# A two-layer graph network on one Trainium2 core: the adjacency loaded and turned by halves of its rows, score rows loaded ahead of W, the first norm's factor put into the exponentials, a PSUM bank for each half at the end

## The chip, the core and the metric

The kernel runs on one core of one Trainium2 chip. The core has five engines with a queue of instructions each, carried out in order: TensorE (PE in the profile; it multiplies a loaded 128x128 matrix with a stream of columns and also transposes), VectorE (DVE), ScalarE (ACT), GpSimd (POOL) and SyncE (SP). They wait for each other through semaphores. DMAs are issued from the queues of SP, ACT and POOL and land some microseconds later. Tiles live in on-chip memory with 128 partitions; PE writes into PSUM, here eight banks of 128x512 float32.

The metric is the time of one execution on the device in microseconds. Before the change it is 1136.07 us, the median of three runs (1135.92 to 1138.34).

## The reference

Batch of 32, 512 nodes, 128 features, one adjacency for all. Layer 0 is an attention over neighbours, layer 1 a gated recurrence of five steps with the same adjacency on both of its inputs. Cut to what matters:

```python
# layer 0
h = max(layernorm(x), 0)
hw = h @ W
e_src, e_dst = hw @ a_src, hw @ a_dst
logits = leaky_relu(e_src[:, :, None] + e_dst[:, None, :], 0.2)
alpha = softmax(logits + where(A > 0, 0, -1e9), axis=-1)
x = x + leaky_relu(alpha @ hw + b, 0.3)
# layer 1
h = max(layernorm(x), 0)
for step in range(5):
    m = A @ h                       # the same for "in" and "out"
    av = concat([m, m])
    u3 = h @ u3_w.T + u3_b
    z = sigmoid(av @ w3_w.T + w3_b + u3)
    r = sigmoid(av @ w4_w.T + w4_b + u3)
    hv = tanh(av @ w5_w.T + w5_b + (r * h) @ u5_w.T + u5_b)
    h = (1 - z) * h + z * hv
x = x + h
```

## The kernel before

**Tiling.** A batch is one tile of 128 partitions x 4 x 128 (`K` = 4 rows of nodes on each partition: node `4p + k`). The adjacency is turned once, into `adjT`, half precision, 128 x 4 x 512. One loop in Python makes all work as a list of tasks: for every batch `layer0(b)`, then `recurrence(b, step, ...)` for the five steps.

**What sets the order.** The kernel carries its own planner, `plan` (L88). Each task names its engine, its estimated duration (`COST`), a due time (`key`), what it needs and the buffers it takes. The planner always takes, among the tasks that can begin first, the one with the earliest key, and the instructions of each engine are then issued in that order and pinned to it. So a key, an estimate or a landing time (`ADJ_LANDS` and the `lands=` arguments) changes the order, never the waits themselves, which semaphores make. Instructions outside tasks (constants, some loads) are not pinned and are placed by the framework's own scheduler. Fillers (`idle`, L442) are matmuls on constants that nobody reads: `FIRST_IDLE` = 27 from the start, `FILL` = 8 from 6.15 us and `IDLE` = 36 from 6.5 us in the planner's time, which it takes where no other PE task can begin.

**The start.** SP issues x of batch 0 (L401), a_dst as a column (L412), the adjacency in one DMA of 1 MB (L415), x of batches 1 and 2, then the weights (L422 and on). ACT's queue issues W (`gw`, L407) and a_src as a column (L408). PE turns W (L456) and multiplies it with both score vectors (`wa_ps`, L463); ACT writes the results as three extra columns of `wrow` (L468 to L471). `prepare_adjacency(c)` (L486) transposes four 128x128 blocks of the landed adjacency into a bank, for `c` = 0 to 3, and ACT or DVE copies the bank into `adjT[:, c]` (L503).

**Layer 0 of a batch.** `relu_layernorm` (L602): statistics on DVE (L621, L629, L630), the power -1/2 on POOL (L650, `rs`), for batch 0 centring and scaling on DVE (L659, L665), for the others one ACT activation for each 128 columns (L687). Turning: `transposed` on PE (L707) with an ACT copy (L712) for the first four batches (`direct`), `blockwise` with a DVE transpose and DMAs on POOL's queue (L729 to L752) for the rest. `product` (L803): h times `wrow` (`hp`, L812), exponentials of the extra columns on ACT (L818), scaling of h·W by the exponential (L825). The row of scores is spread over partitions by PE transposes (`es`, L847) for the first four batches and by DMAs (L872, L885) for the rest. `weigh` (L894) makes the weights `pt` on DVE (L897); for batch 0 this goes by halves of 256 columns (`HALVED`). `average` (L921) multiplies them with h·W on PE (`av`, L928), and DVE normalizes and joins (L955 to L982). A second norm and turn follow (`hN`, `t_b`), and the halves `hi` and `lo` in half precision (L1012, L1014).

**A step of the recurrence** (L1018): `m` from `adjT` with `hi` and `lo` (L1037, 8 matmuls of 128x512), copied by ACT (L1048); r gate (L1056, L1057), tanh on ACT (L1062), r·h on DVE (L1069); z gate (L1077, tanh L1089); candidate (L1100, L1101, tanh L1107); three DVE updates (L1114, L1120, L1123); and the way back to node order, by DMA transposes on SP's queue (L1245), by PE, or by DMAs through memory.

**The last step of the last batch** (`ending`, L1256) goes by two halves of 256 columns: candidate (L1288), tanh (L1295), gated product (L1299), a turn that adds the kept part and the new part in PSUM (`minus`, L1276, and `plus`, L1306), sum with x1 (L1314), store (L1322). Both halves share one bank for the candidate (`v_end`) and one for the turned result (`end`).

**The guard.** A flag that inputs keep the fast path's bounds is computed late and read by every engine (L1350) before the last `BRANCH` = 150 tasks.

## Time and profile before

| what | value |
|---|---|
| median of the runs | 1136.07 us (1135.92 to 1138.34, 3 runs) |
| profiled execution | 1138.11 us |
| its span, first to last instruction | 1136.3 us |
| granted PE clock, mean | 0.999 |
| DMA moved | 104.52 MB |
| adjacency, issue to landing | 7.8 us |
| x of a batch, issue to landing, median | 2.9 us |

The rows of the profile are: an engine's busy time (the union of its instructions' times), groups of equal instructions with their mean duration, and a timeline in which a row "10.06 0.87 DVE L621 ..." gives start, duration, engine, line and tiles; in square brackets stands how long the engine was idle before it and what ended that. Matmuls are pipelined and their ends are modelled: a 128x128 float32 transpose is shown with 0.27 us, but the next one starts 0.11 us later, and a 128x512 float32 product is two rows 0.43 us apart. So PE's time is read from starts. Fillers count as busy.

### The profile page before, as it was taken

What the parts mean: (1) busy time and instruction counts of PE and PEld (TensorE: products, weight loads), DVE (VectorE), ACT (ScalarE), POOL (GpSimd) and SP (SyncE); (2) the same over time, 40 slices, a digit from 0 to 9 for tenths busy, and PEclk for the clock granted to TensorE, in tenths of its full rate; (3) what the DMA queues carried; (4) which work ended last, traced back from release to release, by engine and by line L of the source; (5) the groups of instructions that cost most, each with busy time, mean ns of one, the idle gap of its engine ahead of it and who ended that gap; (6) DMA issues with size and microseconds to landing.
All of it is one profiled execution on the core that took longest, in us unless ns stands there. A gap on an engine that the chain in (4) does not pass through costs nothing.

```text
span 1136.3 us, 14341 instructions
## 1 busy us (share of the span) xinstructions
PE 1128.5 (99%) x4337; PEld 593.3 (52%) x4337; DVE 875.9 (77%) x2002; ACT 661.4 (58%) x1299; POOL 352.3 (31%) x504
## 2 busy tenths in 40 slices
PE   8999999999999999999999999999999999999998
PEld 7665554555455545555545554555555554444444
DVE  7889868887687688779777777889888977655655
ACT  5756656645655565656565556665665565545553
POOL 4255542511421344244134214453644221100000
PEclk9999999999999999999999999999999999999999
DMA  3255454543434553454445444545555343231321
GB/s 107 57 84 104 84 113 89 110 105 74 112 75 97 98 121 76 96 125 103 93 94 105 79 91 111 112 100 110 127 113 103 76 75 84 47 74 29 84 74 67
DMA packets 188498, 104.52 MB, mean 92 GB/s; under 512 B 152192, under 2 KB 167680, under 8 KB 188288
## 3 DMA queue, kind: packets, MB, share of 16 engines
q1 hardware_dynamic: 170512, 66.57, 25.8%
q0 software_dynamic: 17472, 36.79, 17.5%
q8 instruction: 36, 0.59, 0.2%
q14 instruction: 46, 0.38, 0.1%
q10 hardware_dynamic: 432, 0.20, 0.1%
HBM read 39.46 MB, written 30.47 MB: 62 GB/s over the span
## 4 chain that ended last, share of the span: by engine, by line
PE 99%; DMA 1%; DVE 0%; SPq 0%; issue 0%; DVEq 0%
PE m L1037 24%; PE g L1077 12%; PE g L1057 12%; PE g L1056 12%; PE v L1100 12%; PE v L1101 12%; PE av L928 10%; PE hp L812 3%; DMA a_sb<-in_adj_dram 1%; PE idle L443 0%; PE at_ps L494 0%; PE t_b L707 0%; PE es L847 0%; PE t_a L707 0%; PE v_end L1288 0%; PE end L1306 0%
## 5 line engine op out<-in xcount | busy, mean ns | idle before, releaser
L1062 ACT ACTIVATE rs<-g,zrb 128x512 f32<-128x512 f32 x160 | 109.6, 685 | 123.1 <-PE g L1057 122.6
L1114 DVE SCALAR_TENSOR_TENSOR d<-hv,hT 128x512 f32<-128x512 f32 x158 | 108.3, 685 | 93.9 <-ACT hv L1107 92.8
L1107 ACT ACTIVATE hv<-v,vb 128x512 f32<-128x512 f32 x159 | 108.9, 685 | 108.2 <-PE v L1101 108.0
L1069 DVE SCALAR_TENSOR_TENSOR rh<-rs,hT 128x512 f32<-128x512 f32 x160 | 109.4, 685 | 70.5 <-ACT rs L1062 69.8
L1056 PE MATMUL g<-hT,u3T 128*128 128x512 f32 x320 | 163.4, 592 | 0.0
L1057 PE MATMUL g<-mT,w4sT 128*128 128x512 f32 x320 | 163.4, 592 | 0.0
L1077 PE MATMUL g<-mT,w3dT 128*128 128x512 f32 x320 | 162.8, 593 | 0.0
L1100 PE MATMUL v<-mT,w5sT 128*128 128x512 f32 x318 | 162.4, 592 | 0.0
L1101 PE MATMUL v<-rh,u5hT 128*128 128x512 f32 x318 | 162.4, 592 | 0.0
L1037 PE MATMUL m<-adjT,hi 128*128 128x512 f16 x640 | 162.1, 379 | 0.0
L1037 PE MATMUL m<-adjT,lo 128*128 128x512 f16 x640 | 160.7, 379 | 0.0
L650 POOL TENSOR_TENSOR rs_b<-ve_b,mhalf 128x4 f32<-128x4 f32 x32 | 37.0, 1155 | 383.0 <-DVE ve_b L630 184.5
L1089 ACT ACTIVATE zs<-g,zrb 128x512 f32<-128x512 f32 x160 | 109.4, 685 | 67.9 <-PE g L1077 66.4
L1048 ACT COPY mT<-m 128x512 f32<-128x512 f32 x160 | 92.8, 583 | 81.5 <-PE m L1037 79.0
L928 PEld LDWEIGHTS av<-hw,pt 128*128 128x128 f32 x1024 | 123.5, 191 | 21.1 <-issue 17.5
L928 PE MATMUL av<-hw,pt 128*128 128x129 f32 x1024 | 125.0, 275 | 0.1
L1123 DVE SCALAR_TENSOR_TENSOR hT<-d,hT 128x512 f32<-128x512 f32 x158 | 109.3, 692 | 11.9
L1237 ACT CAST hiT<-hT 128x512 f16<-128x512 f32 x128 | 78.9, 616 | 63.7 <-DVE hT L1123 63.2
L1037 PEld LDWEIGHTS <-hi 128*128 128x128 f16 x640 | 62.5, 98 | 99.0 <-issue 45.3
L1120 DVE SCALAR_TENSOR_TENSOR d<-zs,d 128x512 f32<-128x512 f32 x158 | 109.2, 691 | 5.2
L1037 PEld LDWEIGHTS <-lo 128*128 128x128 f16 x640 | 62.6, 98 | 90.5 <-issue 25.3
L1240 DVE TENSOR_TENSOR loT<-hT,hiT 128x512 f16<-128x512 f32 x128 | 87.7, 687 | 17.7 <-ACT hiT L1237 16.4
(141 smaller groups left out, 1354.1 us busy)
## 6 DMA issues: line engine op xcount, KB each, us to landing
x<-in_x_dram SPq DMA_DIRECT2D x32, 256.0 KB, 2.9
out_dram<-res SPq DMA_DIRECT2D x31, 256.0 KB, 2.3
turn_a<-blocks_a POOLq DMA_DIRECT2D x112, 64.0 KB, 2.6
h0T<-turn_a POOLq DMA_DIRECT2D x28, 256.0 KB, 4.0
es<-line POOLq DMA_DIRECT2D x28, 256.0 KB, 3.9
turn_b<-blocks_b POOLq DMA_DIRECT2D x112, 64.0 KB, 2.6
hT<-turn_b POOLq DMA_DIRECT2D x28, 256.0 KB, 3.8
way<-blocks SPq DMA_DIRECT2D x28, 256.0 KB, 2.3
```

Of the source, the lines that this page charges most:

```text
L928: pin(nc.tensor.matmul(avs()[:, i, :], lhsT=f_pts[c].tile[:, ts(2 * part + i, P)], rhs=hw()[:, c, : D + 1], start=start, stop=(c == K - 1) ...
L1037: pin(nc.tensor.matmul(f_m.tile, lhsT=part[:, k, :], rhs=adjT[:, k, :], start=(first and k == 0), stop=(not first and k == K - 1),))
L1056: pin(nc.tensor.matmul(g, lhsT=u3T, rhs=hT, start=True, stop=False))
L1057: pin(nc.tensor.matmul(g, lhsT=w4sT, rhs=f_mT.tile, start=False, stop=True))
L1062: pin(nc.scalar.activation(new(f_r, f"rs_{b}_{step}"), f_g.tile, AF.Tanh, bias=rb, scale=0.5))
L1069: pin(nc.vector.scalar_tensor_tensor(new(f_rh, f"rh_{b}_{step}"), f_r.tile, 1.0, hT, ALU.add, ALU.mult))
L1077: pin(nc.tensor.matmul(f_g.tile, lhsT=w3dT, rhs=f_mT.tile, start=False, stop=True, skip_group_check=True))
L1089: pin(nc.scalar.activation(new(f_z, f"zs_{b}_{step}"), f_g.tile, AF.Tanh, bias=zb, scale=0.5))
L1100: pin(nc.tensor.matmul(v, lhsT=w5sT, rhs=f_mT.tile, start=True, stop=False))
L1101: pin(nc.tensor.matmul(v, lhsT=u5hT, rhs=f_rh.tile, start=False, stop=True))
L1120: pin(nc.vector.scalar_tensor_tensor(d, f_z.tile, 1.0, d, ALU.add, ALU.mult))
L1123: pin(nc.vector.scalar_tensor_tensor(hT, f_d.tile, 0.5, hT, ALU.mult, ALU.add))
```

## The change

The adjacency is loaded by two DMAs, `k` = 0, 1 and `k` = 2, 3 of each partition; x of batch 1 is issued between them. `prepare_adjacency` now transposes, for each half of the rows, two pairs of column blocks, and the copies fill half-width parts of `adjT`. The weights `pt` need only the parts that they read.

The score vectors are loaded as two rows of one tile (`avecs`), issued on ACT's queue ahead of W. A matmul with a constant 2x4 matrix `pick` turns them into four columns (`acols`: a_dst, 0.8 a_src, -0.8 a_dst, a_src), which one product with W's transpose turns into the columns of `wrow`, 16 equal columns each, read back by one ACT copy. `pick` is made by four DVE operations from the identity, outside the planner's tasks.

For batch 0 the first norm is only centred and clipped; its factor `rs` goes into the exponentials as their scale and, times the exponential, into the scaling of h·W. The two halves of batch 0's turned h and of its spread scores have a bank each.

Batch 3's scores are spread and its second norm is turned by DMA now (`DIRECT_E`, `DIRECT_B` = 3). There are 24 fillers instead of 71. In the planner, PE's tasks before 6 us count double, `EARLY` is 7, keys of single tasks are shifted by a table, and landing times are others. The flag is read before the last 110 tasks.

At the end each half has its own bank for the candidate and for the turned result; the gated product is written over `hv`; the stores change queues; the z gate of the last batch no longer stands ahead of batch 30's candidate.

```diff
+DIRECT_A, DIRECT_E, DIRECT_B = 4, 3, 3
...
+SAME = 16
...
-EARLY = 6
+EARLY = 7
...
-ADJ_LANDS = 5600
+ADJ_LANDS = (4100, 5650)
+X_LANDS = (2800, 4450, 6250)
+X_FIRST = 1
+HALF_CLOCK = 6000
...
+BY_DVE = (1, 3)
+UNSCALED = 1
...
+BY_MATMUL = (0, 1)
+Z_AHEAD = 0
+SHIFT = {
+    ('adj', 0): 15.5, ('adj', 3): -1.0, (0, 0, 'step'): 1.5, (0, 18): 2.5, (0, 2, 'step'): -2.0,
...
+}
...
-FIRST_IDLE, FILL, IDLE = 27, 8, 36
+FIRST_IDLE, IDLE = 24, 0
...
-BRANCH = 150
+BRANCH = 110
...
-    acols = prep.tile([P, 2], F32, name="acols")
+    avecs = prep.tile([2, D], F32, name="avecs")
+    acols = prep.tile([P, 4], F32, name="acols")
+    pick = prep.tile([2, 4], F32, name="pick")
+    for i, (row, by) in enumerate(((1, 1.0), (0, 0.8), (1, -0.8), (0, 1.0))):
+        nc.vector.tensor_scalar(
+            pick[:, i : i + 1], ident[0:2, row : row + 1], by, None, ALU.mult
+        )
...
+    weights_0 = prep.tile([P, K], F32, name="weights_0")
...
+    nc.scalar.dma_start(out=avecs[0:1, :], in_=g_asrc.rearrange("(o d) -> o d", o=1))
+    nc.scalar.dma_start(out=avecs[1:2, :], in_=g_adst.rearrange("(o d) -> o d", o=1))
     nc.scalar.dma_start(out=gw, in_=g_w)
-    nc.scalar.dma_start(out=acols[:, 0:1], in_=g_asrc.rearrange("(d o) -> d o", o=1))
...
     def load_rest(name):
-        if name == "a_dst":
-            pin(nc.sync.dma_start(out=acols[:, 1:2], in_=g_adst.rearrange("(d o) -> d o", o=1)))
-            return
-        if name == "a":
-            pin(nc.sync.dma_start(out=a_sb, in_=adj.rearrange("(p k) m -> p k m", k=K)))
+        if isinstance(name, int):
+            ks = slice(2 * name, 2 * name + 2)
+            pin(nc.sync.dma_start(
+                out=a_sb[:, ks, :], in_=adj.rearrange("(p k) m -> p k m", k=K)[:, ks, :]
+            ))
             return
...
+    xs = {0: load_x(0, -9.9e9, X_LANDS[0])}
+    a_loaded = [add("SP", [1], -9.7e9, lambda: load_rest(0), lands=ADJ_LANDS[0])]
+    if X_FIRST:
+        xs[1] = load_x(1, -9.65e9, X_LANDS[1])
+    a_loaded.append(add("SP", [1], -9.6e9, lambda: load_rest(1), lands=ADJ_LANDS[1]))
+    if not X_FIRST:
+        xs[1] = load_x(1, -9.55e9, X_LANDS[1])
+    xs[2] = load_x(2, -9.5e9, X_LANDS[2])
+    rest_loaded = add("SP", [1] * 6, -9.45e9, lambda: load_rest("rest"), (xs[2][1],), lands=3000)
...
-    for n, columns, at in ((FIRST_IDLE, 480, 500), (FILL, 60, 6150), (IDLE, 256, 6500)):
-        for _ in range(n):
...
+    f_ac = Buffer("o", "bank")
     def issue():
-        pin(nc.tensor.matmul(new(f_wa, "wa_ps")[:, 0:2], lhsT=gwT, rhs=acols, start=True, stop=True))
-    t = add("PE", [256], soon, issue, (a_dst_loaded, t), (f_wa,), at=5000)
+        pin(nc.tensor.matmul(
+            new(f_ac, "ac_ps")[:, 0:4], lhsT=avecs, rhs=pick, start=True, stop=True
+        ))
+    u = add("PE", [256], soon, issue, (), (f_ac,), at=4200)
+    u = add("ACT", [1], soon, lambda: pin(nc.scalar.copy(acols, f_ac.tile[:, 0:4])), (u,), (f_ac,))
...
-        pin(nc.scalar.copy(wrow[:, D : D + 1], f_wa.tile[:, 1:2]))
-        pin(nc.scalar.mul(wrow[:, D + 1 : D + 2], f_wa.tile[:, 0:1], 0.8))
-        pin(nc.scalar.mul(wrow[:, D + 2 : D + 3], f_wa.tile[:, 1:2], -0.8))
-        pin(nc.scalar.copy(wa, f_wa.tile[:, 0:2]))
-    wrow_made = wa_made = add("ACT", [1] * 4, soon, issue, (t, w_copied), (f_wa,))
+        pin(nc.tensor.matmul(
+            new(f_wa, "wa_ps")[:, : 4 * SAME].rearrange("p (i q) -> p i q", i=4), lhsT=gwT,
+            rhs=acols.rearrange("p (i o) -> p i o", o=1).to_broadcast([P, 4, SAME]), start=True,
+            stop=True,
+        ))
...
+    t = add("PE", [256], soon, issue, (u, t), (f_wa,), at=0)
...
+    def issue():
+        pin(nc.scalar.copy(wrow[:, D : D + 4], f_wa.tile[:, 0 : 4 * SAME : SAME]))
+    wrow_made = add("ACT", [1], soon, issue, (t, w_copied), (f_wa,))
...
-    def prepare_adjacency(c):
+    def prepare_adjacency(i):
...
-        t = add("PE", [256] * K, key, turn, (a_loaded,), (f,), at=9900 if c > 1 else 0)
-        engine, copy = ("DVE", nc.vector.tensor_copy) if c % 2 else ("ACT", nc.scalar.copy)
-        adjacency.append(
-            add(engine, [512], key, lambda: pin(copy(adjT[:, c, :], f.tile)), (t,), (f,))
-        )
+            new(f, f"at_ps{i}")
+            for k in range(2):
+                for c in range(2):
+                    pin(nc.tensor.transpose(
+                        parts()[:, c, k, :],
+                        a_sb[:, 2 * two + k, :].rearrange("p (q c) -> p c q", c=K)[:, 2 * cs + c, :],
+                        ident,
+                    ))
+        t = add("PE", [256] * K, key, turn, (a_loaded[two],), (f,))
+        engine, copy = ("DVE", nc.vector.tensor_copy) if i in BY_DVE else ("ACT", nc.scalar.copy)
+        adjacency.append(add(
+            engine, [512], key,
+            lambda: pin(copy(
+                adjT[:, 2 * cs : 2 * cs + 2, ts(two, N // 2)],
+                f.tile.rearrange("p (c n) -> p c n", c=2),
+            )),
+            (t,), (f,),
+        ))
...
+            def centre(half):
+                def issue():
+                    for k in (2 * half, 2 * half + 1):
+                        pin(nc.vector.tensor_scalar(
+                            dst()[:, k, :], src()[:, k, :], own["mv"][:, k, 0:1], 0.0,
+                            ALU.subtract, ALU.max,
+                        ))
+                return issue
+            factor.append((own, t))
+            return [add("DVE", [128] * 2, keys(2), centre(i), (t1,), buffers) for i in range(2)]
...
-        f = Buffer("o", "bank")
+        fs = [Buffer("o", "bank")] * 2
+        if by_halves:
+            fs[1] = Buffer("o", "bank")
...
+            two = slice(2 * half, 2 * half + 2)
             def exponentials():
-                pin(nc.scalar.activation(
-                    hw()[:, 2 * half : 2 * half + 2, D:], hp2()[:, :, D:], AF.Exp
+                if unscaled:
+                    for k in range(2 * half, 2 * half + 2):
+                        pin(nc.scalar.activation(
+                            hw()[:, k, D:], hp2()[:, k - 2 * half, D:], AF.Exp,
+                            scale=norm["rs"][:, k : k + 1],
+                        ))
+                    return
+                pin(nc.scalar.activation(hw()[:, two, D:], hp2()[:, :, D:], AF.Exp))
+            def weight():
+                by = norm["rs"][:, two].rearrange("p (k o) -> p k o", o=1)
+                pin(nc.vector.tensor_tensor(
+                    weights_0[:, two].rearrange("p (k o) -> p k o", o=1), hw()[:, two, D : D + 1],
+                    by, ALU.mult,
                 ))
             def scale():
                 for c in range(2):
                     k = 2 * half + c
-                    pin(nc.scalar.mul(hw()[:, k, :D], hp2()[:, c, :D], hw()[:, k, D : D + 1]))
...
+                    by = weights_0[:, k : k + 1] if unscaled else hw()[:, k, D : D + 1]
+                    pin(nc.scalar.mul(hw()[:, k, :D], hp2()[:, c, :D], by))
...
+        if b < DIRECT_E:
+            f_ess = [Buffer("g", "bank")] * 2
+            if by_halves:
+                f_ess[1] = Buffer("o", "bank")
...
+                es_made.append(add("PE", [256] * 2, keys(0), spread(half),
+                                   (made[half], *es_made[-1:]), (f_hw, f_ess[half])))
...
-        def weigh(c, of, key):
+        def parts_of(of, c):
+            return [adjacency[2 * i + c // 2] for i in range(2) if of.start < N // 2 * (i + 1)
+                    and of.stop > N // 2 * i]
...
+            return add("DVE", [of.stop - of.start], key, issue,
+                       (es_made[half], made[c // 2], *parts_of(of, c)), (f_es, f_hw, f_pts[c]))
...
         t = turn(lambda: hTs[b % SLOTS], hN, f"b{b}", keys, t, (f_hN,), False)
-        return halved, t[0] if direct else t
+        return halved, t[0] if b < DIRECT_B else t
...
         if b >= B - LEVEL:
             key = min(key, (5 * B - EARLY - LEVEL * (STEPS - 1 - step)) * STEP)
+        key += SHIFT.get((b, step, "step"), 0) * STEP
...
-        if last and b == B - 1:
+        if Z_AHEAD and last and b == B - 1:
...
+            f = Buffer("o", "bank") if i else f_v
+            by_matmul = i in BY_MATMUL
+            f_end = Buffer("o", "bank") if by_matmul else f
+            of = slice(ks.start * P, ks.stop * P)
+            width = of.stop - of.start
...
             def candidate():
-                v = f_v.tile or new(f_v, f"v_{b}_end")
+                v = new(f, f"v_{b}_end_{i}")
                 for w, src in ((w5sT, f_mT), (u5hT, f_rh)):
...
             def gated():
-                p = f_p.tile or new(f_p, f"gated_{b}")
+                hv = f_hv.tile[:, of]
                 pin(nc.vector.scalar_tensor_tensor(
-                    p[:, ts(i, M)], f_z.tile[:, ts(i, M)], 1.0, f_hv.tile[:, ts(i, M)], ALU.add,
-                    ALU.mult,
+                    hv, f_z.tile[:, of], 1.0, hv, ALU.add, ALU.mult
                 ))
...
+            def turn_kept():
+                new(f_end, f"end_{b}_{i}")
+                for k in range(ks.start, ks.stop):
+                    pin(nc.tensor.matmul(
+                        f_end.tile[:, ts(k - ks.start, P)], lhsT=f_d.tile[:, ts(k, P)], rhs=minus,
+                        start=(k == ks.start), stop=False, skip_group_check=True,
+                    ))
...
-                    ))
+                for k in range(ks.start, ks.stop):
+                    if by_matmul:
+                        pin(nc.tensor.matmul(
+                            f_end.tile[:, ts(k - ks.start, P)], lhsT=f_hv.tile[:, ts(k, P)],
+                            rhs=plus, start=False, stop=True, skip_group_check=True,
+                        ))
...
             def result():
                 res = f_res.tile or new(f_res, f"res_{b}", (P, K, D))
-                ks = slice(two * i, two * i + two)
-                pin(nc.vector.tensor_tensor(
-                    res[:, ks, :], f.tile.rearrange("p (k d) -> p k d", k=K)[:, ks, :],
-                    x1s[b % SLOTS][:, ks, :], ALU.add,
+                pin(nc.vector.scalar_tensor_tensor(
+                    res[:, ks, :], f_end.tile[:, :width].rearrange("p (k d) -> p k d", d=D),
+                    1.0 if by_matmul else 0.5 / LIFT, x1s[b % SLOTS][:, ks, :], ALU.mult, ALU.add,
...
             def store():
-                ks = slice(two * i, two * i + two)
-                queue = nc.sync if i else nc.scalar
+                queue = nc.scalar if STORES[i] == "ACT" else nc.sync
                 pin(queue.dma_start(out=out_r[b][:, ks, :], in_=f_res.tile[:, ks, :]))
...
+            pieces.append(u)
+            key = ENDING_KEY + i
+            u = add("ACT", [width], keys(4 + key), tanh_v, (u,), (f, f_hv))
...
+            if by_matmul:
+                kept = add("PE", [512] * n, keys(-1), turn_kept, (t_keep, pieces[0]), (f_end, f_d))
+                u = add("DVE", [width], keys(4 + key), gated, (u, t_z), (f_z, f_hv))
+                u = add("PE", [512] * n, keys(4 + key), turn, (u, kept), (f_end, f_hv))
...
+            u = add("DVE", [width], keys(5 + key), result, (u,), (f_end, f_res))
+            add(STORES[i], [350 if STORES[i] == "ACT" else 1], keys(5 + key), store, (u,),
+                (f_res,), lands=LANDING)
```

## The prediction

> **What bounds the kernel now.** I read the engine totals and the chain that ended last, then the timeline of the first 40 us, then the load rates by stretch, then the end of the chain.
>
> ```profile
> span 1136.3 us, 14341 instructions
> ...
> PE 1128.5 (99%) x4337; PEld 593.3 (52%) x4337; DVE 875.9 (77%) x2002; ACT 661.4 (58%) x1299; POOL 352.3 (31%) x504
> ...
> PE 99%; DMA 1%; DVE 0%; SPq 0%; issue 0%; DVEq 0%
> ```
>
> TensorE (PE) is busy for all but 7.8 us: 0.8 before its first filler, 2.1 until the adjacency is there, 4.9 at the end. No stretch between 15 us and 1130 us has a hole over 0.05 us. So the time is: start of useful PE work, plus that work, plus fillers, plus what follows the last matmul. The change can only act on the first and last 30 us and on the number of PE instructions. The profiled execution took 1138.11 us: 1136.3 of span and 1.8 around it. The median of the three timed runs, 1136.07, lies 2.04 lower.
>
> ```profile
> 0.78 3.79 PE L443 MATMUL idle<-const-bfloat16-1.0 128*128 128x256 bf16 x17 [0.78 <-PEq L1384]
> 1.66 0.42 SPq L415 DMA_DIRECT2D a_sb<-in_adj_dram  x1
> 5.38 1.95 PE L443 MATMUL idle<-const-bfloat16-1.0 128*128 128x256 bf16 x16
> 9.46 0.75 PE L494 MATMUL at_ps<-ident,a_sb 128*128 128x128 f32 x4 [2.13 <-DMA a_sb<-in_adj_dram]
> 10.06 0.87 DVE L621 BATCH_NORM_STATS2 st_a<-x 128x6 f32<-128x128 f32 x4 [2.67 <-DMA x<-in_x_dram]
> 11.40 0.69 DVE L503 CAST adjT<-at_ps 128x512 f16<-128x512 f32 x1
> 15.01 2.43 DVE L897 SCALAR_TENSOR_TENSOR pt<-es,hw,adjT 128x256 f32<-128x256 f32 x6
> 22.59 2.73 DVE L897 SCALAR_TENSOR_TENSOR pt<-es,hw,adjT 128x512 f32<-128x512 f32 x4
> 32.16 1.12 PE L1077 MATMUL g<-mT,w3dT 128*128 128x512 f32 x2
> ```
>
> PE's first useful work starts at 9.46 us, when the adjacency has landed, 7.75 us after its issue. From 10 to 35 us VectorE (DVE) has hardly a gap, and PE fills its waits with 30 fillers at 0.11 us (3.3 us). The z product at 32.16 us is my milestone: after it PE meets five more fillers and no long wait.
>
> ```profile
> 2.00:3.00 1.00, 1.00 (x7) 0.74 (x5) 0.00 (x0) 0.67 (x2) 0.34 (x1) 1.00 0.66 244
> 3.00:4.00 1.00, 1.00 (x7) 0.69 (x6) 0.33 (x2) 0.00 (x0) 0.00 (x0) 1.00 1.00 249
> 4.00:5.00 1.00, 1.00 (x8) 0.80 (x6) 0.96 (x9) 0.18 (x2) 0.00 (x0) 1.00 0.95 385
> 5.00:6.00 1.00, 1.00 (x11) 0.81 (x9) 0.62 (x2) 0.63 (x6) 0.90 (x1) 1.00 1.00 369
> 6.00:7.00 1.00, 1.00 (x11) 0.88 (x10) 0.48 (x2) 0.00 (x0) 1.00 (x2) 1.00 0.91 344
> ```
>
> The last column is GB/s. With 32 KB moved before 2 us, the running sum is 0.28 MB at 3 us, 0.53 at 4, 0.91 at 5, 1.28 at 6, 1.62 at 7. What stands first (x of batch 0, W, the adjacency: 1.38 MB) was moved by 6.3 us, yet the adjacency counted as landed only at 9.41. I infer that one share of it lagged in this execution and that the 2.04 us to the median are that lag: in a median run it lands at about 7.4, 1.1 us after its bytes.
>
> **The change, part by part.**
>
> *The first wait moves to another load.* The new `ac_ps` matmul stands on PE before the first adjacency transposes. Its operand `pick` comes from four small DVE operations, and in the built program these stand on DVE behind the statistics of x of batch 1. So `ac_ps`, and behind it the transposes of the first half, W's turn, h's turn, all of PE, wait for that x: third on SP's queue now, after x of batch 0 and the first half. Bytes up to it: 0.262 + 0.066 (W) + 0.524 + 0.262 = 1.11 MB, passed at 5.55 us; plus the 1.1 us gives 6.65, less up to 0.46 for being issued one issue earlier; I take 6.3. Bounds: 4.6 (issued at 1.66, plus the 2.9 us that x loads take by the median) and 10.05 (where it landed in the profile). From landing to the next DVE operation the rows give 11.40 - 10.06 = 1.34; four small ones at 0.07 (rows of 128x2 memsets, 0.06) and a write of 0.16 make 1.75. `ac_ps` starts at 8.1, the first transposes after two fillers at 8.45. The first half, landing about 5.4 by the same sum, waits 3 us for nothing.
>
> *From there to z.* PE lines up ac 0.14, fillers 0.22, transposes 0.44, W 0.21, h 0.44, transposes 0.44, fillers 0.22, transposes of the second half 0.44, scores and products 1.1: products done at 11.65. DVE copies the second block at 11.0 to 11.7, takes x of batch 2's statistics (1.4, moved behind it) and starts the weights `pt` of batch 0 at 13.2, for 8 x 0.41 = 3.3, to 16.45. ScalarE's queue has h of batch 1 (4 x 0.40) ahead of the scaling, which still ends at 14.9, before its use. Normalizing, joining, statistics (rows from 17.36 to 21.81: 4.5, less overlap) put batch 1's `pt` at 21.3; with x of batch 3's statistics (1.34) now put inside them, the first recurrence starts at 26.6 and z at 31.8, against 32.16. Two more transposes are done by then (0.22): -0.6. The first norm's factor in the exponentials takes the 0.9 us wait for `rs_a` (L665) out of DVE, but h waited on PE anyway, so it is worth nothing here; likewise the score rows as rows, since `ac_ps` waits longer for `pick`. Behind them on ScalarE's queue W is issued third, near 1.7, and lands near 4.8 (3.1 as now): the same wait covers it; without that wait W's turn would be held to 4.9. SP loses one issue (a_dst) and gains one (a half), so x of batch 2 and the weights are issued when they are now. The bounds of the landing move this term to -2.3 and +3.15.
>
> *Clock.* PE has no work from about 4.6 (18 fillers at 0.21) to 8.1, 3.5 us. The rows: 2.13 us of idling before 9.46 cost nothing that shows (16 transposes at 120 ns start to start, later ones 109). After the last matmul at 1131.7 the granted clock is 1.00, then 0.75 in 1134 to 1135, then 0.50: it fell after some 2.8 us. The first fillers took 0.21 each, those from 5.38 on 0.12. So half rate is possible from 8.1 on; the 3.4 us of PE work up to the products would take up to 1.7 more. Bounds 0 and +1.7. The wait is nearer the row with the fall, but in a part of this stretch PE waits for DVE and ScalarE anyway, and one fall is thin evidence: I take a third, +0.5.
>
> [...]
>
> *PE instructions.* Batch 3's score spread and second turn go to DMA (`DIRECT_E`, `DIRECT_B` 4 to 3): 8 transposes x 0.109 = -0.87. They cost two DVE transposes (0.70 and less), and on POOL's queue 4 + 1 and 4 + 1 DMAs of 2.6 and 3.9 us; POOL is 31% busy, and other batches' recurrences cover them. Without that cover PE would wait some 6.5 us (2.6 + 3.9) once. Fillers after z, 5 x 0.11, go: -0.55, unless a real wait stood there (0).
>
> *The end.*
>
> ```profile
> 1129.04 0.91 PE end L1276 x8
> ...
> 1130.51 1.17 PE end L1306 x8
> 1131.69 0.02 issue
> 1131.71 0.09 DVE res L1314
> 1131.80 0.25 issue
> 1132.05 0.41 DVE res L1314
> ```
>
> Both result halves wait for the last of eight matmuls in one bank. With a bank each, the first half (0.38) is added while the second is turned; but batch 30's result (0.69) now stands on DVE between the two gated halves and holds the second by 0.2 or so. From the last batch's r gate to the last result I count 12.2 against 12.63 now: -0.4 (bounds 0 and -0.76). The stores swap queues; the 3.8 us after the last result stay. Halving the end's loads of banks adds no PE work. The gate z order (`Z_AHEAD` 0), `EARLY` 7 and the key shifts move instructions within a full PE: nothing, as long as what is moved is ready; bound +1.
>
> Sum: -0.6 + 0.5 - 0.87 - 0.55 - 0.4 = -1.9 against the profiled execution's 1138.11, that is **1136.2**. The start term sets a landing without lag (6.3) beside a z row that has the lag, so the sum is for a run without it, like the median of 1136.07: no change.
>
> **Rivals.**
> *Faster: x of batch 1 lands early.* If it lands at the 4.6 that issue and median landing give, the whole start moves 1.7 earlier: 1134.5; with no half-rate clock and the end at its bound (-0.36), 1133.6, and 1132.7 if in addition the waits at 20 to 22 us (1.8 us in my count, where PE waits for batch 1's `pt`) are half filled. For: the rates before 4 us are low only because the first transfers are starting. Against: at the table's rates 0.76 MB is there at 4.6, not 1.11.
> *Slower: x of batch 1 lags like the adjacency did.* Place: `ac_ps`, with all of PE behind it. Landing at 10.05 adds 3.75: 1139.9. It decides from a landing at 8.4, 2.1 later than mine. For: the profile has exactly such a lag, and one of three timed runs (1138.34) looks like it. Against: the median run did not have it.
> *It doesn't do what it says.* The first half isn't used early; that is part of my forecast. If instead `ac_ps` were not held, PE would start near 5.5 and with a start 3 us earlier the time near 1133.
>
> **How the numbers follow.** What a measurement of this kernel can tell from no change is about 0.2%, 2.3 us: 1133.8 to 1138.3. Forecast, no change at 1136.2: 0.48, its own range 1134.2 to 1137.8 (clock and end between their bounds, the landing within 0.7). Faster, by the early landing or the unheld start, about 1133: 0.35. Slower, by the lag: 0.17. The range reaches into the faster cases, where twice as much chance lies, to 1132.2, and to 1138.5 above.
>
> **What would show it.** In the changed profile: the first matmul after the fillers is `ac_ps`, released by DVE's `pick`, near 8 us, and the first transposes follow it at once; DVE's statistics of the second x begin near 6.3. Wrong if transposes start near 5.5. The spacing of transposes after it (0.11 or 0.22) shows the clock. z near 32. At the end the two results stand apart, one before the last turns. Holes on PE between 40 and 1100 us would show the shifts at fault, and I have none.

## The result and the profile after

The changed kernel takes 1139.61 us (median of 20 runs, 1138.17 to 1140.65), the kernel before 1136.51 in 20 runs beside it (1135.8 to 1138.83): a ratio of 1.0022, 95% interval 1.0015 to 1.0029 (estimated over all the runs, so it is not the quotient of the two medians). On a second chip it was 1139.70 against 1138.23 (11 and 33 runs), 1.0015 (1.0004 to 1.0026). So the change makes the kernel slower, by 1.5 to 3.1 us by the medians and 1.7 to 2.5 by the ratios, where 1136.2 and no change were forecast. The kernel before has executions near 1136.4, near 1138.3 and on five of six chips some near 1140.1, in shares that differ from chip to chip, so its median moves by up to 2 us; what follows is compared by ratios on one chip, which these shares also move a little, or by profiles.

The page of the changed kernel: span and totals, and the chain that ended last.

```profile
span 1138.4 us, 14242 instructions
...
PE 1125.7 (99%) x4284; PEld 591.4 (52%) x4284; DVE 872.5 (77%) x2013; ACT 662.8 (58%) x1298; POOL 356.8 (31%) x514
...
PE 96%; DMA 2%; DVE 1%; ACT 0%; issue 0%; SPq 0%; POOL 0%; POOLq 0%
```

PE carries out 53 matmuls fewer, and its share of the chain falls from 99% to 96%: DMA and DVE now have parts of it. The profiled execution took 1140.2 us: 1138.4 of span and 1.8 around it. Where these parts lie is seen in the timeline of the start (start, duration, engine, line, tiles, and in brackets the idle time before and what ended it):

```profile
0.78 3.73 PE L480 MATMUL idle<-const-bfloat16-1.0 128*128 128x256 bf16 x18 [0.78 <-PEq L1521]
...
7.29 0.87 DVE L686 BATCH_NORM_STATS2 st_a<-x 128x6 f32<-128x128 f32 x4 [1.66 <-DMA x<-in_x_dram]
...
8.62 0.32 DVE L416 TENSOR_SCALAR pick<-ident 2x1 f32<-2x1 f32 x4
...
8.99 0.58 PE L501 MATMUL ac_ps<-pick,avecs 2*128 2x4 f32 x2 [4.48 <-DVE pick L416]
...
9.91 1.06 PE L552 MATMUL at_ps<-ident,a_sb 128*128 128x128 f32 x4
...
15.21 0.64 PE L552 MATMUL at_ps<-ident,a_sb 128*128 128x128 f32 x4
...
25.53 2.92 PE L1047 MATMUL av<-hw,pt 128*128 128x129 f32 x24 [1.63 <-DVE pt L1015]
...
35.33 1.12 PE L1199 MATMUL g<-mT,w3dT 128*128 128x512 f32 x2 [0.34 <-ACT rs L1184]
```

The wait stands where it was forecast: x of batch 1 lands, its statistics run, then `pick`, then `ac_ps`, and PE has had nothing to do for 4.48 us. The first half of the adjacency had landed at 6.4 and W at 6.6. And the same four transposes take 1.06 at 9.91 and 0.64 at 15.21. The windows of the start say why (the columns are the stretch, its length, the busy time of the five engines, the granted clock, the DMA share and GB/s):

```profile
6.00:7.00 1.00, 0.00 (x0) 0.00 (x0) 0.00 (x0) 0.00 (x0) 0.00 (x0) 1.00 1.01 355
7.00:8.00 1.00, 0.00 (x0) 0.00 (x0) 0.71 (x4) 0.00 (x0) 0.00 (x0) 0.76 0.98 372
8.00:9.00 1.00, 0.01 (x1) 0.01 (x1) 0.91 (x11) 0.00 (x0) 0.27 (x1) 0.50 1.02 358
9.00:14.00 5.00, 5.00 (x24) 4.86 (x25) 0.69 (x1) 1.71 (x7) 1.99 (x4) 0.50 0.45 109
14.00:15.00 1.00, 1.00 (x10) 1.00 (x9) 0.48 (x1) 0.18 (x1) 0.00 (x0) 0.83 0.00 0
```

The granted clock falls to half at 7.5 us and comes back at 14.3; all of PE's work between 8.99 and 14.3 runs at half speed. In the start of the profile before it stayed at 1.00.

The z product thus starts at 35.33, 3.17 later than before (32.16). From there to the end of the span it is 1138.4 - 35.33 = 1103.07 against 1136.3 - 32.16 = 1104.14: the rest of the kernel gained 1.07. Together they are the 2.1 us between the spans. The end itself:

```profile
1131.85 1.13 PE L1425 MATMUL end<-minus,kept 128*128 128x128 f32 x8
1132.05 0.69 DVE L1340 SCALAR_TENSOR_TENSOR res<-h,x 128x512 f32<-128x512 f32 x1
...
1132.82 1.06 PE L1433 MATMUL end<-plus,hv_end 128*128 128x128 f32 x8
1133.46 0.87 DVE L1444 SCALAR_TENSOR_TENSOR res<-end,x 128x256 f32<-128x256 f32 x2 [0.39 <-PE end L1433]
```

The first half of the result starts at 1133.46 while the second is still being turned (until 1133.88); before, both waited for all eight. Batch 30's result (1132.05) stands between the two gated products, as expected.

### The profile page after: what moved, and what is told of

Read it like the earlier page. It is cut to its first block, busy times and chain, and to the rows that moved or that the text cites. A ratio compares the mean times of both kernels' runs of the same rounds, so it can differ in the third digit from the quotient of the medians.

```text
span 1138.4 us, 14242 instructions
## 1 busy us (share of the span) xinstructions
PE 1125.7 (99%) x4284; PEld 591.4 (52%) x4284; DVE 872.5 (77%) x2013; ACT 662.8 (58%) x1298; POOL 356.8 (31%) x514
## 4 chain that ended last, share of the span: by engine, by line
PE 96%; DMA 2%; DVE 1%; ACT 0%; issue 0%; SPq 0%; POOL 0%; POOLq 0%
PE m L1159 24%; PE g L1199 12%; PE v L1222 12%; PE v L1223 12%; PE g L1178 12%; PE g L1179 12%; PE av L1047 10%; PE hp L896 2%; DMA x<-in_x_dram 0%; DMA lo<-loT 0%; DMA hi<-hiT 0%; DVE pt L1015 0%; DMA es<-line 0%; PE at_ps L552 0%; PE v_end L1402 0%
## 5 line engine op out<-in xcount | busy, mean ns | idle before, releaser
L1179 PEld LDWEIGHTS g<-mT,w4sT 128*128 128x128 f32 x320 | 60.8, 190 | 76.5 <-issue 71.3
```

The lines of the kernel that those rows point to most:

```text
L1179: pin(nc.tensor.matmul(g, lhsT=w4sT, rhs=f_mT.tile, start=False, stop=True))
```

## The experiments

"Transposes" is the start of the first adjacency transposes, "z" that of the first z product, "rest" the span's end less z, all from one profile of each kernel, which is not always of a median run; "half clock" is when the granted clock was 0.5 in it. Ratios are to the kernel before on the same chip.

| kernel | time, us | ratio (95%) | transposes | half clock | z | rest |
|---|---|---|---|---|---|---|
| before, first profile | 1136.51 | 1 | 9.46 | none | 32.16 | 1104.1 |
| before, second profile | 1138.39 | 0.9998 (0.9989 to 1.0007) | 9.39 | 10.5 to 13.9 | 33.71 | 1104.4 |
| before, kept warm | 1137.99 | 0.9997 (0.9988 to 1.0006) | 9.44 | none | 32.14 | 1104.5 |
| changed | 1139.61 | 1.0022 (1.0015 to 1.0029) | 9.91 | 7.5 to 14.3 | 35.33 | 1103.1 |
| changed, other chip | 1139.70 | 1.0015 (1.0004 to 1.0026) | 9.72 | 7.1 to 13.9 | 35.02 | 1102.7 |
| fillers in the wait | 1136.57 | 0.9986 (0.9977 to 0.9995) | 10.21 | none | 33.58 | 1102.0 |
| `pick` early | 1135.12 | 0.9973 (0.9963 to 0.9983) | 6.14 | none | 30.03 | 1103.3 |
| `pick` early, kept warm | 1134.79 | 0.9972 (0.9962 to 0.9981) | 6.36 | none | 30.13 | 1102.6 |
| the same, one load | 1134.60 | 0.9972 (0.9963 to 0.9981) | 6.77 | none | 30.15 | 1103.3 |

**`pick` early.** Nothing but the place of `pick` on DVE: the memset behind it is pinned, so that DVE's statistics come after both.

```diff
-    nc.vector.memset(half, 0.5)
+    pin(nc.vector.memset(half, 0.5))
```

> The changed kernel with the four operations that make `pick` ahead of all statistics on DVE; PE's order is unchanged. Theory (the hold): all of PE stood behind `ac_ps`, `ac_ps` behind `pick`, `pick` behind x of batch 1, and the 4.5 us without work (4.5 to 9.0) let the clock fall to half until 14.3. Then `ac_ps` runs near 4.5, the first transposes begin when the first half and W are there (6.4 and 6.6 in the changed kernel's profile), the idle stretch is about 2 us, the granted clock stays 1.00, the z product comes at 31 to 32 instead of 35.3, and the time is 1135.3 to 1136.3. Rival (the landings of W, x of batch 1 and the second half set the start anyway): z moves less than 1 us, the time stays above 1138.5.

Measured: 1135.12 (9 runs), ratio 0.9973, just below the range given. The timeline of PE's start:

```profile
4.55 0.38 PE L501 MATMUL ac_ps<-pick,avecs 2*128 2x4 f32 x2
...
6.14 0.72 PE L552 MATMUL at_ps<-ident,a_sb 128*128 128x128 f32 x4 [0.88 <-DMA a_sb<-in_adj_dram]
...
20.22 2.92 PE L1047 MATMUL av<-hw,pt 128*128 128x129 f32 x24 [1.61 <-DVE pt L1015]
...
30.03 1.13 PE L1199 MATMUL g<-mT,w3dT 128*128 128x512 f32 x2 [0.34 <-ACT rs L1184]
```

PE now waits for the adjacency's first half alone, 0.88 us; z comes 5.3 us earlier than in the changed kernel, earlier than expected. The 1.61 us that PE waits for batch 1's `pt` are there as before, only earlier. The hold of `ac_ps` is shown as the cause: with one line moved, +0.15% to +0.22% becomes -0.27%. On one chip, the changed kernel took 1139.70 and `pick` early with the eight fillers of a later experiment 1134.79.

**Fillers in the wait.** The wait is left, PE is kept busy in it.

```diff
     def issue():
+        for _ in range(36):
+            idle()
         pin(nc.tensor.matmul(
             new(f_ac, "ac_ps")[:, 0:4], lhsT=avecs, rhs=pick, start=True, stop=True
```

> The changed kernel with 36 more fillers directly ahead of `ac_ps` on PE: the wait stays as it is, only PE is kept busy in it. Theory (the hold costs twice, by the wait and by the clock): `ac_ps` still at 9.0, the granted clock 1.00 from then on, transposes 0.11 apart instead of 0.21, z about 2 us earlier (33.2), time 1137.2 to 1138.0. Rival (the half clock lies beside waits for DVE and ScalarE and costs nothing): z at 35, time 1139.6.

Measured: 1136.57, ratio 0.9986, below the range given. The fillers overran: `ac_ps` started 0.67 later than in the changed kernel, and still z is 1.75 earlier.

```profile
9.66 0.38 PE L503 MATMUL ac_ps<-pick,avecs 2*128 2x4 f32 x2
...
10.21 0.64 PE L554 MATMUL at_ps<-ident,a_sb 128*128 128x128 f32 x4
...
33.58 1.12 PE L1201 MATMUL g<-mT,w3dT 128*128 128x512 f32 x2 [0.34 <-ACT rs L1186]
```

From `ac_ps` to z it is 23.92 here and 26.34 there: the half clock costs 2.42 us of this stretch. In the two other profiles with the wait and the half clock (other chip, no late shifts) it is 26.22 and 26.59. The rival, that it lies beside other waits, is out.

**The changed kernel on another chip**, since the kernel before was 1.9 us slower on the chip of the first experiments.

> The changed kernel as it is, beside the others on one chip, since the kernel before took 1136.5 on the chip of the result and 1138.4 on that of the first experiments. Theory (hold and half clock come from the order of the instructions): the z product again near 35, the clock at half from about 7.3 to 14, time 2.4 to 3.5 above the kernel with fillers in the wait (1136.6 there), that is 1139.0 to 1140.2. Rival (what separated them was the chip): 1137 to 1138.

Measured: 1139.70, z at 35.02, half clock from 7.1 to 13.9. The chip is not the reason.

**Without the late shifts**, alone and with `pick` early.

```diff
-}
+}; SHIFT = {k: v for k, v in SHIFT.items() if k[0] == 'adj' or k[0] < 25}
```

> The changed kernel without the key shifts of batches 25 to 31; everything before 800 us keeps its order. Theory (the late shifts made the holes of 1.24 us that PE has at 903 and 972 us, for late hi and lo): the holes go, the time falls by about 1 us to 1138.6. Rival (the shifts pay for something at the end, or the holes come from the transposes that went to DMA): the same holes or others of that size, 1139.6 or more.

> Both: `pick` early and no late shifts. If the two causes are independent, the gains add: 1134.3 to 1135.3, below the kernel before (1136.5). If one hides the other, it stays at the better of the two.

Measured: 1139.06, ratio 1.0005 (0.9996 to 1.0014), and 1136.09, 0.9980 (0.9971 to 0.9989). In the first the holes at 903 and 972 us are gone, in the second there is one of 0.78 at 1009. But the kernel with fillers in the wait has the late order of the changed kernel and none of these holes either, and others with it have 0.1 to 1.4 us: they are waits for `hi` and `lo` by DMA that come and go. So the shifts are neither cleared nor convicted. The gains did not add, and why the second kernel is 1 us above `pick` early alone isn't settled. Its profiled execution showed something else, in the windows:

```profile
6.00:7.00 1.00, 0.56 (x5) 0.59 (x6) 0.00 (x0) 0.00 (x0) 0.00 (x0) 1.00 1.03 369
7.00:8.00 1.00, 1.00 (x7) 1.00 (x6) 0.53 (x3) 0.56 (x3) 0.00 (x0) 0.50 1.00 382
...
10.00:11.00 1.00, 1.00 (x9) 1.00 (x8) 0.34 (x1) 0.39 (x1) 0.19 (x1) 0.79 0.28 61
```

a half clock from 7.0 to 10.4, after PE had idled for 1.54 us only (the first half landed at 6.3) and was already at work again. The order of the start is that of `pick` early, whose profile had 0.88 us idle there and no such stretch.

**`pick` early, kept warm.** Eight fillers behind `ac_ps` cover that stretch.

```diff
             new(f_ac, "ac_ps")[:, 0:4], lhsT=avecs, rhs=pick, start=True, stop=True
         ))
+        for _ in range(8):
+            idle()
```

> `pick` early, and 8 more fillers directly behind `ac_ps`, which end about when the first half lands (near 6.0). Theory (the idle 1 to 2 us before the first transposes sometimes still lets the clock fall, as in one of the two profiles with `pick` early, from 7.0 to 10.5): no profile and no run with a half clock, the slowest runs (1136.7) go, the median falls by 0.3 to 0.8, from 1135.1 to 1134.3 to 1134.8. Rival (the stretch is too short to matter and the fillers hold the transposes up): 1135.1 or slower.

Measured: 1134.79, ratio 0.9972, on another chip than `pick` early, whose ratio was 0.9973: the median gain is not shown. The spread is 1134.4 to 1135.75 in place of 1134.2 to 1136.7, but that rests on one run of nine, with a mean clock of 0.998. More runs agree: with this start and without the eight fillers (three kernels) 6 of 31 executions have a mean clock under 0.999, with them (this kernel and the one with one load, twice each) none of 46. When the clock fell in them is known for the profiled ones alone. Again, on a third chip:

> The kernel with halves, `pick` early and warm fillers again, on the same chip as the one with one load. Theory (the halves are worth nothing here, since W's turn and x of batch 1 come at 6.5 to 7.2 either way): within 0.3 us of it. Rival (halves are worth some tenths): 0.3 or more below it.

Measured: 1134.46, ratio 0.9979 (0.9970 to 0.9987); the kernel with one load beside it 1134.59.

**Batch 3's way on PE again**, with `pick` early.

```diff
-DIRECT_A, DIRECT_E, DIRECT_B = 4, 3, 3
+DIRECT_A, DIRECT_E, DIRECT_B = 4, 4, 4
```

> `pick` early, but batch 3's scores spread and its second norm turned by PE again (`DIRECT_E`, `DIRECT_B` = 4). Theory (PE is the bound from 20 us on): 8 transposes of 0.109 more, +0.87: 1136.0. Rival (the DMA ways of batch 3 bring waits that cost what the transposes did): 1135.1 or less.

Measured: 1140.33, ratio 1.0019 (1.0009 to 1.0028): both theories miss. In the profiled execution, the slowest (1141.76), PE waits 0.90 for `hi` and then, in the timeline,

```profile
76.58 1.43 PE L1159 MATMUL m<-adjT,lo 128*128 128x512 f16 x4 [2.22 <-DMA lo<-loT]
77.81 1.08 PE L896 MATMUL hp<-wrow,h0T 128*128 128x131 f32 x4
```

after 2.2 us idle the clock falls to half again, from 77.1 to 80.5. With the keys of batch 3 left out of the table as well (and kept warm):

> As `pick` early kept warm, with batch 3's scores and second norm on PE again (`DIRECT_E`, `DIRECT_B` = 4) and without the key shifts of batch 3, which belong to its way by DMA. Theory (the 5 us that direct 4 lost were holes of 1.1, 2.4 and some smaller ones at 70 to 80 us, made by those shifts): the holes shrink, 8 transposes of 0.109 remain: 1135.5 to 1136.5. Rival (the planner's order depends on all shifts together): again above 1138.

Measured: 1139.18, ratio 1.0011 (1.0002 to 1.0020); other holes, 2.7 us between 100 and 104. So the time is the rival's. Its reason, that the order of the first 100 us depends on the shifts and these settings together, fits but isn't tested by itself; in these two tries the 0.87 us of the eight transposes couldn't be separated. Their worth stays a count.

**The old ending**, with `pick` early: `ending` as before, `Z_AHEAD` 1.

> `pick` early, with the ending of the kernel before (one bank for both halves, one store queue order, z gate ahead of batch 30's candidate). Theory (the ending's gain is 0.67 us from batch 30's candidate to the last result less 0.23 us of later stores, read from the two profiles): +0.44: 1135.6. Rival (the stores set the end anyway): 1135.1.

Measured: 1136.76, ratio 0.9994 (0.9984 to 1.0004), more than expected. With one bank for both halves, the planner's order here puts the first half's result between the turns, and the second turns wait for its reading: from the first `v_end` to the last result 5.84 us against 4.65 with separate banks. In the kernel before it was 5.32.

```profile
1127.83 0.42 DVE L1436 TENSOR_TENSOR res<-end,x 128x256 f32<-128x256 f32 x1
...
1128.30 0.71 PE L1428 MATMUL end<-plus,gated 128*128 128x128 f32 x4 [0.59 <-DVE res L1436]
```

But this profile is of the fastest execution, 1135.10, no slower than the profiled one of `pick` early (1135.12), which has 1.2 us of late holes where this one has 0.25. So the longer ending accounts for about 1 us; the rest of the distance to 1136.76 is not shown. Four of the eleven executions have a mean clock of 0.997 or 0.998, and none of them was profiled.

**The kernel before once more**, for its clock and landings.

> The kernel before once more, for a second profile and the granted clock of each of its executions, whose times lie in three groups (1136.5, 1138.4 and 1140.2). The prediction inferred that the profile of 1138.11 had one DMA share late and that a run of 1136.1 to 1136.5 has the adjacency 2 us earlier. If so, a profile of the fast group has the first transposes near 7.5 and z near 30; one of the middle group 9.4 and 32. If both groups show the same landing, the 2 us are elsewhere.

Measured: its executions lie near 1136.6, 1138.3 and 1140.1; the profiled one took 1139.9. The adjacency landed at 9.34, as late as in the first profile. Its windows:

```profile
9.00:10.00 1.00, 0.61 (x5) 0.61 (x6) 0.03 (x1) 0.00 (x0) 0.00 (x0) 1.00 0.18 62
10.00:11.00 1.00, 1.00 (x10) 1.00 (x9) 1.00 (x8) 0.83 (x3) 0.00 (x0) 0.74 0.30 91
11.00:12.00 1.00, 1.00 (x6) 0.76 (x6) 0.93 (x5) 0.31 (x2) 0.59 (x1) 0.50 0.26 56
```

PE had idled 2.5 us until 9.39 and was at work for a microsecond when the clock fell, from 10.5 to 13.9: z at 33.71 instead of 32.16, and this is the slowest group. With 12 fillers ahead of the first transposes:

> The kernel before with 12 more fillers directly ahead of its first adjacency transposes, about 1.4 us of PE's wait for the adjacency. Theory (the clock falls in some of its executions too, and makes the group at 1140.2): that group and the clock of 0.998 go; the fast group, where the adjacency lands before the fillers end, becomes up to 1.3 slower; median 1137.5 to 1138.3. Rival (that group is a still later landing): it stays.

Measured: 1137.99, range 1137.17 to 1138.61; no run is of the slowest group and no mean clock is under 0.999, against 2 of 11 runs of the kernel as it is, and 3 of 27 beside it on that chip, near 1140 with a mean clock of 0.998. Eleven runs are too few to show that the group is gone. The two fastest are 1137.17 and 1137.49, against 1136.61 and 1136.72. The adjacency lands at 9.39 once more.

**One load.** `pick` early, kept warm, but the adjacency in one DMA.

```diff
-            ks = slice(2 * name, 2 * name + 2)
+            if name: return
+            ks = slice(0, K)
```

> `pick` early kept warm, but the adjacency in one DMA again, ahead of x of batch 1; the order of every engine's instructions is that of the kernel with halves. Theory (loading by halves is what lets PE begin at 6.3: the first half lands at 5.9 to 6.4 in every profile of the changed kernels, the whole adjacency at 9.4 in three profiles of the kernel before): the whole lands between 8.4 (where the second half lands now) and 9.4, the first transposes with it, x of batch 1 at 9 to 10; z 2 to 3.5 later, at least one slow group with a half clock, time 1136.8 to 1138.5. Rival (halves are worth nothing, the gain was the score rows and the fillers): below 1135.5.

> The kernel with one load again, for a second profile and a comparison on one chip: the adjacency's shares within 0.6 us of each other, landing 6.0 to 6.6, time 1134.3 to 1135.0.

Measured: 1134.60 and 1134.59, ratios 0.9972 (0.9963 to 0.9981) and 0.9976 (0.9968 to 0.9985): the theory falls, the rival holds. The whole adjacency lands at 6.33 and 6.43, no later than its first half does when loaded by halves (5.9 to 6.5), and 3 us earlier than in the kernel before, which issues the same DMA 0.46 later. The trace has 16 landings for this transfer, called its shares here. With one load and no columns they end within 0.5 us of each other; in the kernel before 2.6 to 3.1, in a first half 1.3 to 2.1. What the kernel before has ahead of it are the loads of a_dst and a_src as columns, 128 elements of 4 bytes each. These were added back, into a tile that nobody reads:

```diff
     nc.scalar.dma_start(out=gw, in_=g_w)
+    nc.scalar.dma_start(out=spare[:, 0:1], in_=g_asrc.rearrange("(d o) -> d o", o=1))
...
             ks = slice(0, K)
+            pin(nc.sync.dma_start(out=spare[:, 1:2], in_=g_adst.rearrange("(d o) -> d o", o=1)))
```

> The kernel with one load, `pick` early and warm fillers, plus the two column loads of the kernel before (a_dst on SP's queue ahead of the adjacency, a_src on ACT's queue behind W) into a tile that nobody reads. Theory (the loads of 128 single elements hold up single shares of the transfers behind them): the shares of the adjacency end 2 to 3 us apart, the last near 8.5 to 9.4, PE waits for it, time 1136.5 to 1138.5. Rival (the drift has another cause): landing near 6.3, 1134.6 as without them.

> The same with only a_dst's column on SP's queue. If the column directly ahead of the adjacency does it: as with both. If the one on ACT's queue: landing near 6.3 and 1134.6. If each costs a part: between.

Measured: 1138.04, ratio 1.0005 (0.9993 to 1.0018), with both, and 1135.89, 0.9992 (0.9983 to 1.0001), with a_dst's alone. The DMA views give the microseconds from issue to landing (last column); first one load without columns (second profile), then both columns added, then one:

```profile
a_sb<-in_adj_dram SPq DMA_DIRECT2D x1, 1024.0 KB, 5.2
```

```profile
a_sb<-in_adj_dram SPq DMA_DIRECT2D x1, 1024.0 KB, 7.9
```

```profile
a_sb<-in_adj_dram SPq DMA_DIRECT2D x1, 1024.0 KB, 5.9
```

And PE's wait for it, with both and with one:

```profile
9.68 1.10 PE L558 MATMUL at_ps<-ident,a_sb 128*128 128x128 f32 x4 [3.43 <-DMA a_sb<-in_adj_dram]
...
7.72 0.99 PE L557 MATMUL at_ps<-ident,a_sb 128*128 128x128 f32 x4 [1.44 <-DMA a_sb<-in_adj_dram]
```

The landings are 6.43, 9.55 and 7.58, the spread of the shares 0.4, 3.1 and 1.1 us. In the second PE idles 3.43 us for the adjacency and the clock is half from 8.0 to 14.8; in the third 1.44 us and from 8.0 to 11.4. So the column loads make the adjacency late, and the medians on one chip follow: 1134.59, 1135.89 with one, 1138.04 with both. Of the 3.1 us, a_dst's brings 1.15 (0.46 of it by a later issue), and a_src's, on another queue and behind W, added to it, the other 2.0. This split rests on one execution of each; a_src's alone was not run. Executions differ: five of the twelve with both took 1135.8 to 1136.9, and whether the adjacency is as late in these isn't known. By which way the columns do it isn't shown.

Of all kernels run, one load with `pick` early and the fillers is as good as any: 0.3% below the kernel before, 0.4% to 0.5% below the changed one by the ratios.

## Why the prediction was wrong

| step | predicted | measured |
|---|---|---|
| x of batch 1 lands | 6.3 | 7.27 |
| from the landing to `ac_ps` | 1.8 | 1.72 |
| `ac_ps` to z, full clock | 23.7 | 23.92 (fillers in the wait) |
| half clock | 0.5 (0 to 1.7) | 2.42 |
| z with the clock | 32.3 | 35.33 |
| end | -0.4 | -0.44 |
| holes by the shifts | 0 (up to 1) | 1.24 in PE at 903 to 974, read from starts; in other kernels 0 to 1.4 |

*The mechanism was right.* `ac_ps` holds PE, released by `pick`, behind the statistics of x of batch 1. With `ac_ps` at 8.99 in place of 8.1 (0.9), the clock at 2.4 in place of 0.5 (1.9) and 0.2 more to z, the whole 3.0 us by which z missed are found.

*The step that failed most is the clock.* "I take a third, +0.5" was chosen from one stretch of 2.13 us that cost nothing and one fall 2.8 us after the last matmul. The measured cost lies above the upper bound of 1.7, because that bound took only the 3.4 us of work up to the products as exposed; PE worked 5.4 us at half speed (8.99 to 14.34). Other than after the last matmul, the clock was at half in eight profiles, for 3.4 us (10.5 to 13.9, 7.0 to 10.4, 8.0 to 11.4, 77.1 to 80.5) or for 6.8 (7.5 to 14.3, 7.1 to 13.9, 7.8 to 14.6, 8.0 to 14.8). PE had idled 1.44 to 2.51 us where it lasted 3.4, and 3.43 to 4.49 us where it lasted 6.8; 2.13 us in the kernel before had no fall. So the wait, forecast at 3.5 us of idling and measured at 4.48, was of the longer kind. Of the two rows that the prediction had, the fall after 2.8 us was the one to go by, and it should have had the larger weight.

*The second is the landing.* The bytes were there near 6.0 by the rates of the changed kernel (1.13 MB), later than the 5.55 taken from the rates before, and the last share came 1.3 later, where the forecast left 0.75 (6.3 less 5.55).

*The third is a reading of the profile before.* The late adjacency was taken for a lag of one execution. It was at 9.3 to 9.4 in all three profiles of that kernel, and adding the column loads brings it back (9.55). So the score rows, priced at nothing "since `ac_ps` waits longer for `pick`", are the part that has a worth: they bring the whole adjacency from 9.4 to 6.3. In the changed kernel it came to nothing, because `ac_ps` waits longer for `pick`. The halves, first in the change's title, are worth nothing that can be measured once `pick` is early (1134.46 with them, 1134.59 without).

*The rivals.* "Slower: x of batch 1 lags" had the right place and nearly the time (1139.9), by another price: x was 1 us late, short of the 8.4 from which it was to decide, and the clock did the rest. That the time agrees is luck. The unheld start, "near 1133", is what `pick` early tests: 1135.1, and 1134.5 to 1134.8 kept warm. PE began its transposes there at 6.14, not at 5.5.

*The end and the rest* were near. From batch 30's second candidate product to the last result it is 5.50 without the z gate that now stands between (1134.33 - 1127.97 - 0.86), against 6.18; the stores end 0.24 later after it: -0.44. The rest after z without late holes is 1101.9 to 1102.2 in four profiles, 2.0 to 2.3 below before, against -2.04 forecast (-0.87, -0.55, -0.4, and -0.22 for two transposes done before z). With the late holes it was -1.07. So of the 4.0 us between the forecast change of the profiled execution (-1.9) and the measured one (+2.1), 3.0 stand before z and 1.0 behind it. The single terms for the transposes and the fillers weren't separated.

*What stays open.* Why some executions of the kernel before take 1136.5: none of them was profiled, so the earlier landing in them, from which the prediction reckoned its 1136.2, is unproven; with 12 fillers its fastest run is 1137.2, which would fit. And the executions of the changed kernel price the clock lower than the profiles: the eleven of 20 with a mean clock of 0.997, that of the profiled one with its 6.8 us of half clock, took 1139.9 by their median, and the four with 1.000 took 1138.5, only 1.4 less, and still 2 us above the kernel with fillers in the wait (1136.57, on another chip). Of the other five, one (0.998) took 1138.35 and four (0.999) 1139.4 to 1140.0. No execution at 0.998 or above was profiled, so what else holds these up is open.

## What to carry to other kernels

A small operation that is left to a scheduler can stand behind a load that it has nothing to do with, and hold a whole engine, here PE for 4.48 us: look up what stands ahead of each new operand on its engine, then pin it. Price a wait of PE twice, by its length and by the clock: here idle stretches from 1.44 us up were followed by a clock of 0.50 for 3.4 or 6.8 us, though 2.13 us in one profile were not, and eight fillers in a wait cost nothing that shows (ratio 0.9972 against 0.9973). Try loading vectors as rows where a large transfer is under way: here two loads of 128 single elements each made a 1 MB transfer land 3.1 us later.

## What the runs showed of the hardware

- Other than after the last matmul, the granted clock was 0.50 in eight profiles, for 3.4 us in four and 6.8 us in four. The length of an idle stretch alone did not tell whether it fell: 2.13 us idle before 9.46 were followed by no fall in one profile, 1.44 and 1.54 us by one in two others. In the four profiles with 3.4 us the clock fell 0.3 to 1.1 us after PE had resumed, in the four with 6.8 us while PE was still idle.
- In one profiled execution, two loads of 512 bytes as columns delayed a 1 MB transfer by 3.1 us (0.46 of it by a later issue) and spread the ends of its 16 shares from 0.4 to 3.1 us.
- The shares of the first half end 1.3 to 2.1 us apart with no column loads present, those of the whole in one load 0.4 to 0.5. This wasn't followed further.
